# Stores moved to ScalarE's queue, other rooms for down's first left tiles, and a full-height last contraction tile

## The chip, the cores and the metric

The kernel runs on one core of one Trainium2 chip. The metric is device time in microseconds from the start to the end of the one launch; less is better. A core has five engines that work side by side and meet at semaphores: TensorE (PE, with its weight loads PEld), VectorE (DVE), ScalarE (ACT), GpSimd (POOL) and SyncE (SP), which does nothing here but start DMAs. Each engine takes its instructions in the order in which the program lists them; an instruction that has to wait holds up all that stand behind it on its engine.

## The reference

One transformer layer on a sequence of 2048 rows and 1024 columns: attention and a gated feed-forward network, each between two layer norms, each added to its input. The weights of the feed-forward network are 4-bit codes that are looked up in a table of 16 values and multiplied by a scale for each block of 64.

```
x = x + layernorm(attn(layernorm(x), Wq, Wk, Wv, Wo))       # 16 heads of 64, rotary, causal softmax
x = x + layernorm(ffn(layernorm(x), gate, up, down))

ffn(x):  W = NF4[codes] * scales          # gate, up: 2752 x 1024; down: 1024 x 2752
         inter = silu(x @ Wg.T) * (x @ Wu.T)
         return inter @ Wd.T
```

All data are float32. The dimension of 2752 is 21 tiles of 128 and one of 64.

## The kernel before

Every matrix operand is kept as a high and a low part (`split`, L119: a copy on ScalarE at L120, a subtraction on VectorE at L121), and a product is three matmuls (`mm3`, L112: high x high, high x low, low x high, L114 to L116). The order on each engine comes from a scheduler that simulates the program with its own times, not from the order of the source text. Buffers are slots of nine tags with a fixed number each (`SLOTS`, L70); a tile that wants a slot waits until the former owner's last reader is done. PSUM has eight banks in four tags.

The stages:

- Queries, keys and values are made for 8 pairs of heads and parked in memory; heads attend one after the other. For a head and a quarter J of the rows, `scores` gives unnormalized probabilities (prob, L267, L289) and `weighted` transposes them (pt, L299) and multiplies them with the values (o, L303 and L304). Its result `ol` (L306 on ScalarE, L307 on VectorE) is stored to `at[J]` at L308.
- The last pair of heads runs together with the projection by Wo. `project(t, y, beside)` handles 128 rows: it loads the attended values `af` (L435), splits them to the left operand (a2, in the views a), multiplies (pj, L445 to L447) and copies the result to `y` (L448). `residual` (L450) loads x, normalizes y (L144, on ScalarE), adds it to x on GpSimd (L455), stores the sum to `x1d` (L456) and normalizes it again into y (L144). `project_out` stores that to `yd[t]` (L475); `fill_x2` (L477) loads it back, transposes it and splits it to the operand of the gate and up products. There are 16 row tiles; the first four are done beside the attention.
- `looked_up` (L486) turns codes into weights: it loads a tile of codes (L494) and two of scales (L495, L496), converts (L499), draws five lines through the codes on ScalarE (L504, L506) and combines them on VectorE (L510 to L514). In the projection it is called for the first gate and up tiles with its codes in the single buffer of tag "ol" and its scales in "t2". Later the two share a slot of tag "pw" (3 slots of 4 KB).
- Gate and up: 22 tiles of the inner dimension times four quarters of the rows. `gate_up` (L554) makes two products in PSUM banks, Silu on ScalarE (L574), the product with up on VectorE (L575), and sums and differences on GpSimd (L587 to L595) for a Strassen-Winograd scheme of 7 products, all stored. The last of the 22 tiles has 64 rows; the other half of its tile is set to zero (L573). `down_weights` does the like for the looked-up down weights (L611 zeroes, L614 stores).
- Down: the 7 products, each 11 contraction tiles (kt) times 8 banks (r). `fetch` (L651) loads a left tile `ast` (L654) and, for every second kt, a right tile `bst` (L660), and splits both. In the last product the last four contraction tiles are held back, so that the eight banks end one after the other; `evict` (L700) and `finish` (L682) add, normalize and store. The `finish` calls of the last but one product load their rows of `x1d` (L685) into "pw".

All DMAs are started by SP (`load`, L61), stores too. A store that waits for its data so holds up the loads behind it. The scheduler also lets a DMA wait for the DMA eight places before it.

The rows that the last contraction tile uses before the change (L732, L667):

```python
rows = D if kt == half - 1 and b in ("B21", "B22", "T4") else P
...
a = ab[0][:rows, :, r // 4, r % 4 * P : (r % 4 + 1) * P]
mm3(o, a, ab[1][:rows], first, last)
```

Of the kernel before, what the change touches and what calls it, by code (L numbers as in the profile page):

```python
# [10 lines left out]
F32 = mybir.dt.float32  # L11
# [11 lines left out]
D = 64  # L23
I = 2752
P = 128
KE = E // P
# [31 lines left out]
def block_kernel(ctx, tc, x, wq, wk, wv, wo, gu_codes, gu_scales, d_codes, d_scales, cos_sin, out):  # L58
    nc = tc.nc
    V, A, G, T = nc.vector, nc.scalar, nc.gpsimd, nc.tensor  # L60
    load = nc.sync.dma_start  # L61

    const = ctx.enter_context(tc.tile_pool(name="const", bufs=1))
    small = ctx.enter_context(tc.tile_pool(name="small", bufs=4))
# [9 lines left out]
    def slot(tag, shape, dtype, name):  # L74
        assert int(np.prod(shape[1:])) * 4 <= SLOTS[tag][1] * 1024, (tag, shape)
        return sb.tile(shape, dtype, tag=tag, name=name, bufs=SLOTS[tag][0])

    def bank(tag, name="bk"):
        return ps.tile([P, 512], F32, tag=tag, name=name, bufs=BANKS[tag])
# [3 lines left out]
    def any_bank():  # L83
        turn[0] += 1
        return bank(BANK_ORDER[turn[0] % 8])
# [26 lines left out]
    def mm3(o, w, xx, first, last):  # L112

        r = T.matmul(o, lhsT=w[:, 0], rhs=xx[:, 0], start=first, stop=False)  # L114
        T.matmul(o, lhsT=w[:, 0], rhs=xx[:, 1], start=False, stop=False)  # L115
        T.matmul(o, lhsT=w[:, 1], rhs=xx[:, 0], start=False, stop=last)  # L116
        return r

    def split(hi, lo, src):  # L119
        A.copy(hi, src)  # L120
        V.tensor_tensor(lo, src, f32(hi), ALU.subtract)  # L121

    def ln_stats(row):
        st = small.tile([P, 2, 6], F32, tag="st", name="st")
        for i in range(2):
            V.bn_stats(st[:, i, :], row[i])
        return ln_rest(st)

    def ln_rest(st):
        mv = small.tile([P, 2], F32, tag="mv", name="mv")  # L130
        V.bn_aggr(mv, st.rearrange("p a b -> p (a b)"))
        ve = small.tile([P, 1], F32, tag="ve", name="ve")
        V.tensor_scalar(ve, mv[:, 1:2], EPS, None, ALU.add)
        rs = small.tile([P, 1], F32, tag="rs", name="rs")
        G.tensor_tensor(rs, ve, nhalf, ALU.pow)
        nb = small.tile([P, 1], F32, tag="nb", name="nb")
        V.tensor_scalar(nb, mv[:, 0:1], rs, -1.0, ALU.mult, ALU.mult)
        return mv[:, 0:1], rs, nb

    def halves(row):  # L140
        return row[:, :512], row[:, 512:]

    def normalize(dst, src, stats):
        A.activation(dst, src, AF.Identity, bias=stats[2], scale=stats[1])  # L144
# [12 lines left out]
    yd = [dram.tile([P, E], F32, tag=f"yd{t}", name=f"yd{t}") for t in range(NT)]  # L157
# [3 lines left out]
    at = [dram.tile([E, 512], F32, tag=f"at{c}", name=f"at{c}") for c in range(NC)]  # L161
    x1d = dram.tile([S, E], F32, tag="x1d", name="x1d")
    half = NIT // 2
# [44 lines left out]
    def prep_qkv(m, tags=("w", "w", "w")):  # L208
        return [prep_w(w, m, sc, tag) for w, sc, tag in zip((wq, wk, wv), (0.125, 1.0, 1.0), tags)]
# [82 lines left out]
    def weighted(h, J, prob, v):  # L292
        o = bank("O", "o")
        nk = 4 * J + 4
        for kb in range(nk):
            j0 = max(0, kb - 4 * J)
            pt = bank("T", "pt")
            for j in range(j0, 4):
                T.transpose(pt[:, j * P : (j + 1) * P], prob[kb // 4][:, j, kb % 4 * P : (kb % 4 + 1) * P], ident)  # L299
            cs = slice(j0 * P, 512)  # L300
            pw = slot("pw", [P, 2, 512], FR, "pw")
            split(pw[:, 0, cs], pw[:, 1, cs], pt[:, cs])
            T.matmul(o[:, cs], lhsT=v[:, kb, :], rhs=pw[:, 0, cs], start=kb == 0, stop=False)  # L303
            T.matmul(o[:, cs], lhsT=v[:, kb, :], rhs=pw[:, 1, cs], start=False, stop=kb == nk - 1)  # L304
        ol = slot("ol", [D, 512], F32, "ol")
        A.copy(ol, o[D:P, :])  # L306
        V.tensor_tensor(ol, o[:D, :], ol, ALU.add)  # L307
        load(at[J][h * D : (h + 1) * D, :], ol)  # L308

    def load_kv(h, k, v, cs):  # L310

# [11 lines left out]
    def early(f, *args):  # L323
        tc.trace_state.cur_priority -= EARLY
        r = f(*args)
        tc.trace_state.cur_priority += EARLY
        return r

    xs = [early(make_x, 0)]
    first = [early(prep_qkv, 0), prep_qkv(1, ("pa", "pa", "pb"))]  # L330
# [23 lines left out]
    def attend(h, J, q, k, v, anchors):  # L354
        weighted(h, J, scores(J, q, k, anchors), v)
# [76 lines left out]
    def project(t, y, beside):  # L432

        af = slot("f4", [P, KE, P], F32, "af")
        load(af, at[t // 4][:, t % 4 * P : (t % 4 + 1) * P].rearrange("(k p) n -> p k n", p=P))  # L435
        if beside:
            a2 = [slot("f4", [P, KE, P], FR, "a2") for _ in range(2)]
        else:
            a2 = slot("pa" if t % 2 else "hd", [P, 2, KE, P], FR, "a2")
            a2 = [a2[:, 0], a2[:, 1]]  # L440
        split(*a2, af)
        for n in range(2):
            o = bank("F" if beside else "FSS"[(2 * t + n) % 3], "pj")
            for k in range(KE):
                T.matmul(o, lhsT=a2[0][:, k], rhs=wot[k][n][:, 0], start=k == 0, stop=False)  # L445
                T.matmul(o, lhsT=a2[0][:, k], rhs=wot[k][n][:, 1], start=False, stop=False)  # L446
                T.matmul(o, lhsT=a2[1][:, k], rhs=wot[k][n][:, 0], start=False, stop=k == KE - 1)  # L447
            A.copy(y[:, n * 512 : (n + 1) * 512], o)  # L448

    def residual(t, y, xt):  # L450

        rows = slice(t * P, (t + 1) * P)
        load(xt, x[rows, :])
        normalize(y, y, ln_stats(halves(y)))
        G.tensor_tensor(xt, xt, y, ALU.add)  # L455
        load(x1d[rows, :], xt)  # L456
        normalize(y, xt, ln_stats(halves(xt)))

    x2, x2t = {}, {}

# [10 lines left out]
    def project_out(t, beside):  # L471
        y = slot("pb" if beside else "pw", [P, E], F32, "y")
        project(t, y, beside)
        residual(t, y, slot("f4" if beside else "pb", [P, E], F32, "x1"))
        load(yd[t], y)  # L475

    def fill_x2(t):  # L477
        y = slot("pw", [P, E], F32, "y")
# [3 lines left out]
    for t in range(BESIDE):  # L482
        project_out(t, True)
# [50 lines left out]
    for t in range(BESIDE, NEWX):  # L534
        project_out(t, False)
# [5 lines left out]
    for t in range(NEWX, NT):  # L541
        project_out(t, False)
        if fills:
            fill_x2(fills.pop(0))
        if t >= 10 and steps:
            steps.pop(0)()
# [101 lines left out]
    LAST = 4  # L648
    quarter, b_tile = {}, {}

    def fetch(a, b, kt):  # L651

        st = slot("f4", [P, 2, 512], F32, "ast")
        load(st, aq[a][kt])  # L654
        ta = slot("hd", [P, 2, 2, 512], FR, "at")
        split(ta[:, 0], ta[:, 1], st)
        if kt % 2 == 0:
            n = min(2, half - kt)
            st = slot("pb", [P, 2, 512], F32, "bst")[:, :n]
            load(st, bq[b][:, kt : kt + n])  # L660
            b_tile[b] = slot("w", [P, 2, 2, 512], FR, "bt")
            split(b_tile[b][:, 0, :n], b_tile[b][:, 1, :n], st)
        return ta, b_tile[b][:, :, kt % 2]

    def down(o, ab, r, rows, first, last):

        a = ab[0][:rows, :, r // 4, r % 4 * P : (r % 4 + 1) * P]  # L667
        mm3(o, a, ab[1][:rows], first, last)

    def quarters(name, tag):  # L670
        for _ in range(2):
            t = slot(tag, [P, 4, 512], F32, name)
            quarter.setdefault(name, []).extend([t[:, i] for i in range(4)])
# [51 lines left out]
    for n, (a, b) in enumerate(PRODUCTS):  # L725
        os = [any_bank() for _ in range(8)]
        if n in (0, 1, 3, 4):
            quarters(*(("u", "xc"), ("c", "xc"), None, ("v", "pa"), ("d", "pa"))[n])
        final, held = n == len(PRODUCTS) - 1, []
        for kt in range(half):  # L730
            ab = fetch(a, b, kt)
            rows = D if kt == half - 1 and b in ("B21", "B22", "T4") else P  # L732
            if final and kt >= half - LAST:
                held.append((ab, rows))
                continue
            for r in range(8):
                down(os[r], ab, r, rows, kt == 0, kt == half - 1)
        for r in range(8):
            for i, (ab, rows) in enumerate(held):
                down(os[r], ab, r, rows, False, i == LAST - 1)  # L740
            evict(n, r, os[r])


# [47 lines left out]
```

## Time and profile before

| what | us |
|---|---|
| median of 3 runs | 3069.32 (3069.14, 3069.32, 3074.55) |
| profiled execution | 3075.66 |
| its span in the trace | 3073.8 |
| mean granted clock of TensorE in it | 0.982 of full |

The profile is of one execution, not of the median one. Of the DMA issues that the change touches, the page gives these (data, queue, count, size of one, median time from issue to landing):

```profile
ast<-A SPq DMA_DIRECT2D x33, 512.0 KB, 4.4
```

and for the stretch of the last pair and the projection, 1360 to 1720 us:

```profile
x1d<-x SPq DMA_DIRECT2D x16, 512.0 KB, 4.3
yd<-y SPq DMA_DIRECT2D x16, 512.0 KB, 3.0
...
at<-ol SPq DMA_DIRECT2D x9, 128.0 KB, 2.7
```

In lines of engines, "x" gives the number of instructions merged into one row, the square brackets the idle time of the engine just before it and what ended that. SPq is the queue of SP.

### The profile page before, as it was taken

The numbers are of one execution on the slowest core, as the hardware profiler recorded it, in microseconds if no ns is written. First come the engines' busy times: TensorE is split into PE (matmuls) and PEld (weight loads), VectorE is DVE, ScalarE is ACT, GpSimd is POOL, SyncE is SP. The second block draws the span as 40 slices with busy tenths as digits, with TensorE's granted clock in tenths as the row PEclk, the third lists the DMA queues.
The fourth block names the chain that finished last, engine by engine and source line by source line (L and its number), as shares of the span: only waits on it lengthen the run. The fifth ranks groups of instructions, "written<-read, shape, count | busy, mean of one in ns | idle before, by whom it ended". The sixth has DMA issues, their size and how long they took to land.

```text
span 3073.8 us, 42810 instructions
## 1 busy us (share of the span) xinstructions
PE 2958.1 (96%) x14424; PEld 2426.6 (79%) x14424; DVE 2045.6 (67%) x3920; ACT 1700.1 (55%) x3565; POOL 960.4 (31%) x1055
## 2 busy tenths in 40 slices
PE   7979999999999999999989999999999999999998
PEld 6868888787777787777778788888888888788886
DVE  7556778777777777777565577766666677344347
ACT  3246667676666666666554466555555566332234
POOL 5334444344434343445323112222112223100034
PEclk9989999999999999999999999999999999999999
DMA  8776665747656558463346444344334444644446
GB/s 307 259 223 219 225 217 170 221 151 194 188 182 186 152 199 260 132 198 108 114 152 209 138 143 148 132 136 142 120 133 137 136 153 148 237 140 151 147 141 229
DMA packets 271739, 536.02 MB, mean 174 GB/s; under 512 B 22944, under 2 KB 113056, under 8 KB 255648
## 3 DMA queue, kind: packets, MB, share of 16 engines
q1 hardware_dynamic: 271520, 533.29, 53.8%
q8 instruction: 114, 1.87, 0.2%
q14 instruction: 105, 0.86, 0.1%
HBM read 371.98 MB, written 161.22 MB: 173 GB/s over the span
## 4 chain that ended last, share of the span: by engine, by line
PE 83%; DMA 8%; DVE 4%; ACT 2%; issue 1%; POOL 1%; SPq 1%; POOLq 0%; ACTq 0%; DVEq 0%
PE bk L114 14%; PE bk L115 14%; PE bk L116 14%; PE pt L299 6%; PE qkv L114 6%; PE qkv L115 5%; PE qkv L116 5%; PE o L304 4%; PE s L260 3%; PE o L303 3%; PE s L262 3%; DMA wf<-in_wq 1%; PE pj L445 1%; PE pj L447 1%; PE pj L446 1%
## 5 line engine op out<-in xcount | busy, mean ns | idle before, releaser
L115 PE MATMUL bk<-x,wt 128*128 128x512 f32 x1376 | 536.1, 390 | 0.0
L116 PE MATMUL bk<-x,wt 128*128 128x512 f32 x1376 | 535.8, 389 | 0.0
L114 PE MATMUL bk<-x,wt 128*128 128x512 f32 x1376 | 534.5, 390 | 0.9 <-ACT wt L120 0.9
L289 POOL TENSOR_SCALAR prob<-prob,rc 128x512 f32<-128x512 f32 (+3 forms) x640 | 405.4, 654 | 407.5 <-DVE rc L284 238.8
L267 ACT ACTIVATE prob<-s,mxs 128x512 f32<-128x512 f32 (+3 forms) x640 | 400.9, 629 | 159.1 <-DVE mxs L266 144.8
L121 DVE TENSOR_TENSOR pw<-pt,pw 128x512 fp32r<-128x512 f32 (+3 forms) x640 | 377.4, 602 | 131.2 <-ACT pw L120 129.5
L266 DVE TENSOR_REDUCE mxs<-s 128x1 f32<-128x512 f32 (+3 forms) x640 | 380.0, 602 | 100.5 <-PE s L262 60.2
L506 ACT ACTIVATE ln<-cs,bias 128x512 f32<-128x512 f32 x520 | 359.7, 716 | 109.4 <-DVE m L513 23.0
L120 ACT CAST pw<-pt 128x512 fp32r<-128x512 f32 (+3 forms) x640 | 323.1, 525 | 164.2 <-PE pt L299 134.9
L299 PE MATMUL pt<-ident,prob 128*128 128x128 f32 x2176 | 346.5, 276 | 3.2 <-DVE pw L121 3.0
L299 PEld LDWEIGHTS pt<-ident,prob 128*128 128x128 f32 x2176 | 267.9, 142 | 57.3 <-issue 4.4
L260 PE MATMUL s<-k,q 128*128 128x512 f32 (+3 forms) x640 | 268.7, 420 | 38.1 <-ACT prob L267 36.2
L114 PEld LDWEIGHTS bk<-x,wt 128*128 128x128 f32 x1376 | 258.8, 188 | 55.4 <-ACT wt L120 1.7
L116 PEld LDWEIGHTS bk<-x,wt 128*128 128x128 f32 x1376 | 258.5, 188 | 54.1 <-DVE wt L121 0.5
L115 PEld LDWEIGHTS bk<-x,wt 128*128 128x128 f32 x1376 | 258.6, 188 | 53.7
L304 PE MATMUL o<-pw,v 128*128 128x512 f32 (+3 forms) x640 | 250.3, 393 | 5.3 <-DVE pw L121 4.7
L303 PE MATMUL o<-pw,v 128*128 128x512 f32 (+3 forms) x640 | 246.7, 386 | 4.6 <-ACT pw L120 3.7
L114 PE MATMUL qkv<-xc,w 128*128 128x512 f32 x576 | 237.0, 411 | 13.6 <-ACT w L178 9.1
L114 PE MATMUL bk<-bt,at 128*128 128x512 f32 (+1 forms) x616 | 242.1, 395 | 4.3 <-ACT in L574 4.1
L115 PE MATMUL bk<-bt,at 128*128 128x512 f32 (+1 forms) x616 | 240.7, 391 | 0.0
L116 PE MATMUL bk<-bt,at 128*128 128x512 f32 (+1 forms) x616 | 239.8, 391 | 0.0
L262 PE MATMUL s<-k,q 128*128 128x512 f32 (+3 forms) x640 | 238.6, 374 | 0.0
(145 smaller groups left out, 5478.9 us busy)
## 6 DMA issues: line engine op xcount, KB each, us to landing
xc<-xd SPq DMA_DIRECT2D x96, 1024.0 KB, 8.9
q<-qs SPq DMA_DIRECT2D x128, 256.0 KB, 7.0
ast<-S SPq DMA_DIRECT2D x44, 512.0 KB, 4.0
cs<-in_gu_scales SPq DMA_DIRECT2D x172, 128.0 KB, 3.2
cs<-in_gu_codes SPq DMA_DIRECT2D x86, 256.0 KB, 2.9
A<-in SPq DMA_DIRECT2D x66, 256.0 KB, 2.1
S<-in SPq DMA_DIRECT2D x66, 256.0 KB, 3.1
ast<-A SPq DMA_DIRECT2D x33, 512.0 KB, 4.4
```

The source lines that it names most:

```text
L114: r = T.matmul(o, lhsT=w[:, 0], rhs=xx[:, 0], start=first, stop=False)
L115: T.matmul(o, lhsT=w[:, 0], rhs=xx[:, 1], start=False, stop=False)
L116: T.matmul(o, lhsT=w[:, 1], rhs=xx[:, 0], start=False, stop=last)
L121: V.tensor_tensor(lo, src, f32(hi), ALU.subtract)
L260: mm = T.matmul(s, lhsT=q[:, 0, j * P : (j + 1) * P], rhs=k[:, b:e], start=True, stop=False)
L266: V.tensor_reduce(mx, s, AX.X, ALU.max, negate=True)
L267: A.activation(prob[i][:, j, : e - b], s, AF.Exp, bias=mx, accum_out=sums[:, j % BATCH, i : i + 1])
L289: G.tensor_scalar(p, p, rc[:, jj % BATCH, i : i + 1], 0.0, ALU.mult, ALU.add)
L299: T.transpose(pt[:, j * P : (j + 1) * P], prob[kb // 4][:, j, kb % 4 * P : (kb % 4 + 1) * P], ident)
L303: T.matmul(o[:, cs], lhsT=v[:, kb, :], rhs=pw[:, 0, cs], start=kb == 0, stop=False)
L304: T.matmul(o[:, cs], lhsT=v[:, kb, :], rhs=pw[:, 1, cs], start=False, stop=kb == nk - 1)
L506: A.activation(ln, c8, AF.Prelu, bias=bias_of[ab], scale=ab[0], alpha=ab[2])
```

## The change

It has three parts. The stores of the projection (x1d, yd) and those of the attended values of the last two heads are started by ScalarE's queue; the store of x1d moves behind the second normalization in the source text. The first three left tiles of the first down product are loaded into slots of tag "pw" instead of "f4". The last contraction tile of down always uses all 128 rows, of which 64 are zeros in the short one.

```diff
-    load = nc.sync.dma_start
+    load, store = nc.sync.dma_start, nc.scalar.dma_start
...
-        load(at[J][h * D : (h + 1) * D, :], ol)
+        (store if h >= 2 * KE - 2 else load)(at[J][h * D : (h + 1) * D, :], ol)
...
         G.tensor_tensor(xt, xt, y, ALU.add)
-        load(x1d[rows, :], xt)
         normalize(y, xt, ln_stats(halves(xt)))
+        store(x1d[rows, :], xt)
...
         residual(t, y, slot("f4" if beside else "pb", [P, E], F32, "x1"))
-        load(yd[t], y)
+        store(yd[t], y)
...
-        st = slot("f4", [P, 2, 512], F32, "ast")
+        st = slot("pw" if a == "A11" and kt < 3 else "f4", [P, 2, 512], F32, "ast")
...
-    def down(o, ab, r, rows, first, last):
-
-        a = ab[0][:rows, :, r // 4, r % 4 * P : (r % 4 + 1) * P]
-        mm3(o, a, ab[1][:rows], first, last)
+    def down(o, ab, r, first, last):
+
+        mm3(o, ab[0][:, :, r // 4, r % 4 * P : (r % 4 + 1) * P], ab[1], first, last)
...
-            rows = D if kt == half - 1 and b in ("B21", "B22", "T4") else P
             if final and kt >= half - LAST:
-                held.append((ab, rows))
+                held.append(ab)
                 continue
             for r in range(8):
-                down(os[r], ab, r, rows, kt == 0, kt == half - 1)
+                down(os[r], ab, r, kt == 0, kt == half - 1)
         for r in range(8):
-            for i, (ab, rows) in enumerate(held):
-                down(os[r], ab, r, rows, False, i == LAST - 1)
+            for i, ab in enumerate(held):
+                down(os[r], ab, r, False, i == LAST - 1)
             evict(n, r, os[r])
```

On the queues, 40 DMAs go from SP to ScalarE: 8 of the attended values, 16 of x1d, 16 of yd. The scheduler lays out the work of all engines anew around the projection and around the start of down.

## The prediction

> **What bounds the kernel now.** I read the page first (busy shares, the 40 slices), then the busy time of each engine by stage, then, inside the stages that the diff touches, the instructions of TensorE in order of time with the idle time before each, and last the chain of waits and the queues of SP and ScalarE around each hole.
>
> The page's first two parts, and the busy time by stage (stretch, length, then busy microseconds and instructions of PE, PEld, DVE, ACT and POOL, then clock, DMA share, GB/s):
>
> ```profile
> span 3073.8 us, 42810 instructions
> ...
> PE 2958.1 (96%) x14424; PEld 2426.6 (79%) x14424; DVE 2045.6 (67%) x3920; ACT 1700.1 (55%) x3565; POOL 960.4 (31%) x1055
> ```
>
> ```profile
> 1360.00:1720.00 360.00, 330.48 (x1622) 269.59 (x1621) 229.06 (x507) 212.83 (x427) 123.03 (x126) 0.96 0.46 152
> 1720.00:2540.00 820.00, 820.00 (x3619) 679.00 (x3618) 560.81 (x828) 455.76 (x713) 171.11 (x111) 1.00 0.41 135
> 2540.00:2660.00 120.00, 114.75 (x490) 93.16 (x489) 80.22 (x100) 63.67 (x91) 36.93 (x27) 0.97 0.62 211
> 2660.00:3050.00 390.00, 390.00 (x1712) 319.84 (x1711) 177.31 (x208) 124.30 (x140) 46.73 (x36) 1.00 0.50 158
> ```
>
> TensorE is the bound: it is never idle through the gate and up products and through the down products. So a cover elsewhere is worth nothing; only its holes, its clock and its own instructions count. Its holes lie where the diff works: 29.5 us in the last pair and the projection (1360 to 1720), 5.3 us where down begins (2540 to 2660). The largest, from the instructions of TensorE in order of time (start, length, instruction, idle before it and its releaser):
>
> ```profile
> 1573.99 0.80 PE L445 MATMUL pj<-wo,a 128*128 128x512 f32 x1 [3.84 <-ACT y L448]
> 1589.71 0.79 PE L445 MATMUL pj<-wo,a 128*128 128x512 f32 x1 [6.24 <-ACT a L120]
> 2643.06 0.80 PE L114 MATMUL bk<-bt,at 128*128 128x512 f32 x1 [4.14 <-ACT in L574]
> 2643.65 0.63 PE L115 MATMUL bk<-bt,at 128*128 128x512 f32 x1
> ```
>
> After such a hole the next matmuls start 0.43 us apart instead of 0.227: between 2643.06 and 2648.34 there are 12 of them, 5.28 us in place of 2.72, so the hole costs another 2.6 us.
>
> Third, the starts inside down, where one product changes to its 64-row tile and back:
>
> ```profile
> 2754.34 0.39 PE L116 MATMUL bk<-bt,at 128*128 128x512 f32 x1
> 2754.65 0.49 PE L114 MATMUL bk<-bt,at 64*128 64x512 f32 x1
> 2754.99 0.39 PE L115 MATMUL bk<-bt,at 64*128 64x512 f32 x1
> 2755.22 0.39 PE L116 MATMUL bk<-bt,at 64*128 64x512 f32 x1
> ```
>
> Starts that should be 0.227 apart are 0.31 and 0.34 apart: a change of row count costs 0.2 us, although no idle time is shown. Last, the queue of SP in the projection (who waited for whom, total us, times, longest) and the chain of waits behind the three holes (start, length, what):
>
> ```profile
> SPq L475 <- ACT y L144: 51.8, 11, 7.4
> SPq L308 <- DVE nb L137: 32.2, 1, 32.2
> SPq L308 <- DVE ol L307: 29.0, 5, 12.7
> SPq L456 <- POOL x L455: 24.8, 11, 7.8
> ```
>
> ```profile
> 1565.68 5.91 DMA cs<-in_gu_codes
> ...
> 1581.23 4.22 DMA cs<-in_gu_codes
> ```
>
> ```profile
> 2619.67 5.30 DMA bst<-B
> ...
> 2627.38 3.59 DMA bst<-B
> ...
> 2633.33 6.46 DMA bst<-B
> ```
>
> SP stands some 138 us in front of stores with loads behind them, but the two holes of the projection end on code tables: ScalarE stands in order before a lookup line (L506), and evictions (L448) and left-tile copies (L120) stand behind it. The hole at 2643 ends on the third right tile of down (bst): its copy L120 holds up the last Silu (L574), which must free a PSUM bank.
>
> **What the Trainium skill says.** "DMA: Bandwidth & Descriptors", section "Issuing engines are not separate DMA queues": starting DMAs from several engines saves only the sequencer's time to start them. Agrees as far as it can be seen: a store takes SP 0.32 to 0.57 us. "TensorE: Matmul & The Clock Gate", section "What's actually happening": after an idle window of about 3.4 us the array runs at half clock until it was busy as long. The trace agrees: 0.43 for 0.227 after 4.14 us idle, while the stretch 1480 to 1500, with a hole of 1.65 us, shows clock 1.00. "TensorEngine Tiling (Array Packing)", section "Key Properties": a change of tiling mode drains TensorE. I read a 64-row matmul between 128-row ones as such a change; the 0.2 us fit[...]; here the 64-row L115 takes 388 ns, the 128-row one 389.
>
> **The change, part by part.**
>
> *128 rows for the last contraction tile.* 3 products x 8 x 3 = 72 matmuls keep their length and lose the changes. In the second product and in the sixth the tile comes once for all eight r: one change in, one out, 2 x 0.2 = 0.4 us each. In the last product four tiles are held back and each r goes through 128, 128, 128, 64: its rounds start 3.15 us apart where 12 x 0.227 = 2.72 would do, 0.43 each, 7.5 rounds = 3.2 us. Sum 4.0. The rows added were set to zero before being stored (L573, L611), so no instruction is added. At the end the eight finishes must follow faster: VectorE does 2.4 to 3.1 us per round, so it may lag; I give back 0.4. Value -3.6, ends -4.1 and -2.0.
>
> *The first three left tiles of down in the lookups' rooms (pw).* In the new order of SP they take the places of the three x1 loads (L685, at 2601.6, 2606.1 and 2611.6 before), and these follow. So three loads and splits leave the crowded 2618 to 2636 (DMA share 0.79 to 0.96). Against it: one split is put inside the last lookup on VectorE (1.23 us) and ScalarE (1.05), and SP now waits with its third x1 load until the third tile is split (landing near 2616.5, copies until 2618.8) with T4, S4 and the first right tile behind it: that goes out near 2621.8 in place of 2619.67. Then each right tile needs its load, 1.05 of ScalarE and 1.23 of VectorE before the next may enter the one free pb room: 2629, then 2635.4, landing near 2640 if the load takes 4.5 us and not 6.46. Its copy, then L572 and L574 (0.58 and 0.59) end near 2642. TensorE gets there, as before, at 2638.9. So the hole shrinks by 1 to 2 us, to a length at which the clock may or may not drop (2.6 us). Value -2.2; ends -7.1 (hole and clock loss gone) and +2 (the chain of right tiles late by the whole 2.1 us).
>
> *The stores.* 8 at L308 (heads 14 and 15, four J), 16 at L456 and 16 at L475, 40 DMAs, go from SP's queue to ScalarE's, each with its wait. Issue: 40 x 0.36 = 14 us on ScalarE, which is busy 213 of 360 us; beside TensorE's work except in the chain to the two holes. The waits: L308 for VectorE's sum, 0.7 us; L475 for ScalarE's own L144, nothing; the x1d store for POOL's L455, 2.4 us after L144. Behind it stand ScalarE's casts and evictions, and TensorE for those. In the new order it mostly has lookup lines or evictions ahead of it, or the second L144 behind it, which waits for that sum anyway.
> What is gained: in the chain to 1573.99 the fifth line of the first lookup now comes before the two L144 (2.28 us), so the next codes can go out at 1563.5 and not 1565.68; but a third line (0.7) and a store (0.35) now come before the eviction. Net -1.3 at the first hole. At the second, two L144 and one store more stand before the copy of the left tile, but the whole lookup ahead of it is earlier by some 4 us; I take another -1.3. The rest of the codes' wait stays: their room is one buffer, freed only by the last line. Holes between 1490 and 1515 (1.65, 0.58, 1.70): the left tiles' f4 rooms are freed by TensorE, not by SP, so -0.4. The holes at 1704 to 1710 (1.34, 0.79, 2.22) wait for splits of the last normalized rows, whose loads stood behind the last yd store (1692.62): -1.0. Sum -4.0. Ends: -15.7 (both large holes, 10.1, and two clock losses, 5.2, with 0.4 more) and +10 (rival below).
>
> Sum -3.6 - 2.2 - 4.0 = -9.8. The profiled execution took 3075.66 (span 3073.8 and 1.9 around it) and would take 3065.9; it lies 6.3 above the median of the runs, 3069.32, so the forecast on the median is 3059.5.
>
> **Rivals.** *Everything opens*: without stores SP feeds both lookups early enough and down starts without a stop: -15.7, -7.1 and -4.1, 3042. For it: 138 us of SP's waits. Against: the codes' room and the pb room are not SP's matter. *Only the row change counts*: holes move and keep their size, -3.6, 3065.7, too little to be told from no change. For it: ScalarE's order holds the same lines before the same copies. *Slower*: x1d stores block ScalarE. Some of them (t = 8 and 10, nearly so 13) stand directly behind the L144 whose sum they await, with transposes' copies behind them; 2.5 us each, and from 1600 to 1700 TensorE has almost no hole now (0.56 us). If ten of the projections lose 2.5 us and 60% reaches TensorE through full transpose banks, +15, less the -5.8 of the other two parts: 3078.5. It decides from the point where these holes pass some 12 us in sum. Against: evictions have three banks and 5.4 us per half row tile.
>
> **How the numbers follow.** 0.2%, 6.1 us, is what a measurement of this kernel can tell. Forecast (3054 to 3063) 0.53; everything opens (below 3054) 0.15; only the row change (3063 to 3070) 0.15; slower 0.17, of it 0.03 within 0.2%. So faster 0.68, same 0.18, slower 0.14. Range 3046 to 3072: below it only the far end of the first rival, above it two thirds of the last.
>
> **What would show it.** Right: starts at the last tile 0.227 apart and rounds of 2.72 us in the last product; a hole before the eighth bank of down under 3.5 us; holes near 1574 and 1590 still there but smaller by some 2.6 us in sum; SP without waits on L144. Wrong: holes from 1600 to 1700 behind copies that stand behind a store; the first right tile later than 2623; an end after the last matmul longer by over 2 us, which would mean that the finishes, not the matmuls, set the end.

## The result, and the profile after

| | before | after |
|---|---|---|
| median, us (runs) | 3069.32 (5 runs, 3064.85 to 3075.65) | 3085.6 (5 runs, 3076.7 to 3086.57) |
| ratio after/before, 95% interval | | 1.0042 (1.0022 to 1.0062) |
| profiled execution: span, us | 3073.8 | 3083.8 |
| granted clock | 0.982 | 0.981 |

The changed kernel is slower by 0.42% in the mean of its runs, some 13 us (the medians lie 16 apart); forecast was 9.8 us faster, and the range ended at 3072. The busy time by stage of the changed kernel (stretch, length, then busy time and instructions of PE, PEld, DVE, ACT, POOL, then clock, DMA share, GB/s) shows the two places that the prediction worked on:

```profile
1360.00:1720.00 360.00, 317.67 (x1554) 256.76 (x1553) 212.60 (x482) 201.28 (x401) 120.18 (x124) 0.95 0.46 149
2540.00:2660.00 120.00, 111.29 (x481) 90.78 (x481) 77.82 (x98) 61.04 (x89) 35.65 (x26) 0.97 0.56 186
```

TensorE does 317.67 us in the last pair and the projection where it did 330.48, and 111.29 where down begins in place of 114.75. (These stretches are fixed in time and so don't hold quite the same work: the kernel of the first experiment below, whose projection is unchanged, does 326.40 in the first.) Its instructions in order of time (start, length, instruction, idle before it and its releaser) say where the holes are:

```profile
1569.51 0.50 PE L445 MATMUL pj<-wo,a 128*128 128x512 f32 x1 [3.30 <-ACT y L448]
...
1582.49 1.94 PE L151 MATMUL pt<-ident,y 128*128 128x128 f32 x8 [5.62 <-DMA y<-yd]
1587.04 0.80 PE L445 MATMUL pj<-wo,a 128*128 128x512 f32 x1 [2.61 <-ACT a L120]
...
1649.08 1.94 PE L151 MATMUL pt<-ident,y 128*128 128x128 f32 x8 [7.57 <-DMA y<-yd]
...
2656.73 0.79 PE L114 MATMUL bk<-bt,at 128*128 128x512 f32 x1 [7.61 <-ACT in L574]
```

The first hole is 3.30 where it was 3.84. Forecast was 1.3 less; five traces with the projection of before (named below) show 3.40 to 4.22 there, so little of it is left. The second has another owner: TensorE first waits for rows that are read back from memory (y<-yd), and only then, more briefly, for a left tile. The hole of 7.57 at 1649 is new; at that place the kernel before stood 0.56 us, and the five traces show 0.56 to 2.46. The hole of down grew from 4.14 to 7.61. Only the last product went as forecast: its last three matmuls start 0.23 apart, with no other form among them.

```profile
3071.75 0.39 PE L114 MATMUL bk<-bt,at 128*128 128x512 f32 x1
3071.98 0.39 PE L115 MATMUL bk<-bt,at 128*128 128x512 f32 x1
3072.20 0.39 PE L116 MATMUL bk<-bt,at 128*128 128x512 f32 x1
```

Medians of this kernel move by several us from one set of runs to the next, and the traces show a part of it: one and the same matmul near 1380 (L303, 128x128) starts between 1375.56 and 1387.76 in the traces of kernels whose edits all lie behind it. So I cut each span at four events of TensorE: that matmul; the end of the last transposes of rows read back (L151, near 1710); the arrival at the hole of down (the start of the matmul behind it less its idle time); the start of the last matmul. Those of these lines that aren't shown above, before and then after:

```profile
1381.16 0.33 PE L303 MATMUL o<-pw,v 128*128 128x128 f32 x1 [2.85 <-ACT pw L120]
...
1709.53 0.77 PE L151 MATMUL pt<-ident,y 128*128 128x128 f32 x4 [2.22 <-DVE x L121]
...
3063.15 0.39 PE L116 MATMUL bk<-bt,at 64*128 64x512 f32 x1
```

```profile
1377.00 0.33 PE L303 MATMUL o<-pw,v 128*128 128x128 f32 x1 [3.10 <-ACT pw L120]
...
1720.14 1.06 PE L151 MATMUL pt<-ident,y 128*128 128x128 f32 x4
```

Worked out from them:

| us | up to 1380 | last pair and projection | gate, up | hole of down | down | after the last matmul |
|---|---|---|---|---|---|---|
| before | 1381.2 | 329.1 | 928.6 | 4.1 | 420.1 | 10.7 |
| after | 1377.0 | 344.2 | 927.9 | 7.6 | 415.5 | 11.6 |
| difference | -4.2 | +15.1 | -0.7 | +3.5 | -4.6 | +0.9 |

In five traces whose projection is that of the kernel before (its own, and four from below: the 128 rows alone, the left tiles' rooms alone, these with GpSimd's order held, and the right tiles in pw rooms), this stage takes 327.2 to 333.6 us, 329.9 in the mean, and the idle times of TensorE in it sum to 25.5 to 28.7; in the changed kernel they sum to 38.0. Against that mean the projection lost 14.3, down's beginning 3.5, and the last tile brought 3.7 (4.6 less 0.9).

### The profile page after: what moved, and what is told of

It reads as the page before. It is cut to its first block, busy times and chain, and to the rows that moved or that the text cites. A ratio compares the mean times of both kernels' runs of the same rounds, so it can differ in the third digit from the quotient of the medians.

```text
span 3083.8 us, 42799 instructions
## 1 busy us (share of the span) xinstructions
PE 2953.7 (96%) x14424; PEld 2427.1 (79%) x14424; DVE 2045.1 (66%) x3920; ACT 1700.9 (55%) x3565; POOL 960.0 (31%) x1055
## 4 chain that ended last, share of the span: by engine, by line
PE 79%; DMA 10%; DVE 5%; ACT 2%; issue 2%; POOL 1%; SPq 1%; POOLq 0%; ACTq 0%; DVEq 0%
PE bk L114 13%; PE bk L115 13%; PE bk L116 13%; PE pt L299 6%; PE qkv L114 5%; PE qkv L116 5%; PE qkv L115 5%; PE o L304 4%; PE s L260 3%; PE o L303 3%; PE s L262 3%; DMA xc<-xd 1%; DMA wf<-in_wq 1%; PE pj L445 1%; PE pj L446 1%
## 5 line engine op out<-in xcount | busy, mean ns | idle before, releaser
L121 DVE TENSOR_TENSOR pw<-pt,pw 128x512 fp32r<-128x512 f32 (+3 forms) x640 | 377.2, 601 | 125.7 <-ACT pw L120 123.9
L303 PE MATMUL o<-pw,v 128*128 128x512 f32 (+3 forms) x640 | 246.9, 387 | 4.7 <-ACT pw L120 4.1
L114 PE MATMUL bk<-bt,at 128*128 128x512 f32 x616 | 239.9, 391 | 7.6 <-ACT in L574 7.6
L115 PE MATMUL bk<-bt,at 128*128 128x512 f32 x616 | 240.8, 391 | 0.8 <-DVE bt L121 0.8
L116 PE MATMUL bk<-bt,at 128*128 128x512 f32 x616 | 239.7, 391 | 0.0
```

## The experiments

Each comparison is with runs of the kernel before on the same chip, whose median lay between 3071.4 and 3074.8; 0.1% is 3.1 us.

**The three parts alone.** The rows edit as in the change:

```diff
-            rows = D if kt == half - 1 and b in ("B21", "B22", "T4") else P
-                down(os[r], ab, r, rows, kt == 0, kt == half - 1)
+                down(os[r], ab, r, kt == 0, kt == half - 1)
```

> Only the last contraction tile over 128 rows is taken from the change. Theory A (each part acts alone: rows gain, stores and rooms lose): 3 to 4 us faster, about 3065.5 against 3069; in the last product rounds of 2.72 us and starts 0.227 apart, nothing else moves before 2740 us. Theory B (the row changes cost nothing that reaches the end, since the finishes set it): no change in time, and the idle time after TensorE's last matmul longer by 3 us. If it is slower, the profile's 0.2 us for a change of row count was read wrongly.

Ratio 0.9987 (0.9977 to 0.9996): 4 us faster. Seven rounds of the last product, from the starts of its last 85 matmuls, take 19.04 us where they took 22.07 before, 2.72 each in place of 3.15. Down takes 415.7 in place of 420.1, the end after the last matmul 11.15 in place of 10.65. Theory A.

The rooms of the left tiles:

```diff
-        st = slot("f4", [P, 2, 512], F32, "ast")
+        st = slot("pw" if a == "A11" and kt < 3 else "f4", [P, 2, 512], F32, "ast")
```

> Only the rooms of down's first three left tiles are taken from the change. Theory A (SP's queue: the x1 loads and left-tile splits now stand ahead of the right tiles): 3 to 5 us slower, about 3073, with the hole before the eighth bank of down at 7 us or more in place of 4.14 and the first right tile some 5 us later than 2619.67. Theory B (that delay in the changed kernel came from the stages before, not from the rooms): no change or up to 3 us faster, hole under 4.2 us.

Ratio 1.0012 (1.0003 to 1.0021), 3.7 us slower. The trace shows the chain, from all engines in order of time; gate and up end some 4.5 us earlier in it than in the trace of before (TensorE reaches the hole at 2634.42 and not at 2638.92):

```profile
2602.34 1.84 POOL L623 TENSOR_TENSOR mb<-mb 128x512 f32<-128x512 f32 x1
2602.94 2.32 DVE L121 TENSOR_TENSOR at<-ast,at 128x1024 fp32r<-128x1024 f32 x1
...
2608.28 0.68 DVE L514 TENSOR_TENSOR mb<-mb,cs 128x512 f32<-128x512 f32 x1
...
2608.44 2.82 POOL L591 TENSOR_TENSOR in<-in 128x512 f32<-128x512 f32 x1 [2.02 <-DVE in L575]
2608.88 1.21 DVE L121 TENSOR_TENSOR at<-ast,at 128x1024 fp32r<-128x1024 f32 x1
...
2611.31 0.52 POOL L611 MEMSET mb<- 64x512 f32 x1
2612.17 0.41 SPq L614 DMA_DIRECT2D B<-mb  x1
2618.09 1.29 POOL L629 TENSOR_TENSOR mb<-mb 128x512 f32<-128x512 f32 x1 [4.00 <-DMA B<-mb]
2621.06 0.38 SPq L660 DMA_DIRECT2D bst<-B  x1
...
2642.11 0.80 PE L114 MATMUL bk<-bt,at 128*128 128x512 f32 x1 [7.69 <-ACT in L574]
```

The same steps before:

```profile
2611.69 0.52 POOL L611 MEMSET mb<- 64x512 f32 x1 [1.40 <-DVE mb L514]
2612.24 0.32 SPq L614 DMA_DIRECT2D B<-mb  x1
2612.30 1.62 POOL L591 TENSOR_TENSOR in<-in 128x512 f32<-128x512 f32 x1
...
2616.50 1.28 POOL L629 TENSOR_TENSOR mb<-mb 128x512 f32<-128x512 f32 x1 [1.21 <-DMA B<-mb]
```

The split of a left tile (L121, the part on VectorE), put inside the last lookup, takes 2.32 us in place of the usual 1.21, with GpSimd's subtractions (L623 and the next) beside it. The lookup (its last line is L514) ends 1.9 us later against TensorE's arrival at the hole (25.46 us ahead of it, 27.35 before). GpSimd is then in a sum of the gate tiles (L591), which the scheduler had put behind the zeroing (L611) before; the store of B21 goes out 4.4 us late, lands in 5.9 us in place of 4.26 (why, stays open: an x1 load of 512 KB went out shortly ahead of it in both kernels), and the first right tile goes out 5.9 us late (13.36 us ahead of TensorE's arrival, 19.25 before). Two more right tiles hang on it, through one free room.

All stores on ScalarE's queue, without the other two parts:

```diff
-        load(at[J][h * D : (h + 1) * D, :], ol)
+        (store if h >= 2 * KE - 2 else load)(at[J][h * D : (h + 1) * D, :], ol)
...
-        load(x1d[rows, :], xt)
         normalize(y, xt, ln_stats(halves(xt)))
+        store(x1d[rows, :], xt)
...
-        load(yd[t], y)
+        store(yd[t], y)
```

> Only the moved stores are taken from the change (all three kinds, with the x1d store behind the second normalization). Theory A (the stores make all of the loss in the projection): 10 to 15 us slower, about 3081, with a hole of 5 to 8 us near 1650 in front of the transposes of rows read back from yd, and down beginning as in the kernel before (hole about 4.1 us). Theory B (the loss is shared between the parts or is a matter of single executions): at most 5 us slower and no hole over 3 us between 1600 and 1700.

Ratio 1.0039 (1.0024 to 1.0055), 12 us slower; last pair and projection 343.1 us, hole of down 3.37. The same new hole stands in front of the transposes:

```profile
1593.54 1.94 PE L151 MATMUL pt<-ident,y 128*128 128x128 f32 x8 [5.51 <-DMA y<-yd]
...
1660.82 1.94 PE L151 MATMUL pt<-ident,y 128*128 128x128 f32 x8 [7.94 <-DMA y<-yd]
```

The three parts sum to -4.0 + 3.7 + 12.0 = 11.7 us, the whole change measured 13 (6.8 to 19): they add, as far as the intervals tell. What remains is why the stores cost so much.

**Which stores.** One kind at a time, the edits as above.

> Only the stores of yd (16) go to ScalarE's queue; those of the last attended values and of x1d stay with SP, x1d in its old place. Theory A1 (a yd store on ScalarE's queue lands late, 6.3 us in place of 3.0, and the load of the same row behind it makes TensorE wait): most of the loss of all stores, 8 to 13 us slower, with the hole at 1650. Theory A2 (the x1d store stands in ScalarE's order or in the queue in front of yd and is what delays it): at most 3 us slower here, no hole over 4 us between 1600 and 1700.

> Only the stores of the last pair's attended values (8) go to ScalarE's queue. Theory A1 (what costs is a store of yd that shares the transfers with SP's loads): these are 128 KB and early, so no change within 3 us. Theory A2 (anything that stands in ScalarE's order delays the evictions): 3 to 5 us slower, and with the others' shares the sum of 12.

> Only the x1d stores (16) go to ScalarE's queue, behind the second normalization in the text. Theory A1 (the landing of yd counts, and yd stays in SP's queue in front of the next x load): no change or up to 3 us slower, no hole over 4 us between 1640 and 1660. Theory A2 (the x1d store in ScalarE's order, waiting for GpSimd's sum, is what makes the rows late): 4 to 8 us slower, with second normalizations later by some 5 us against the matmuls of their tile.

| stores on ScalarE's queue | ratio (interval) | us | last pair and projection, us |
|---|---|---|---|
| yd | 1.0014 (1.0003 to 1.0025) | +4.3 | 336.6 |
| at | 1.0009 (1.0000 to 1.0018) | +2.8 | 332.1 |
| x1d | 0.9995 (0.9981 to 1.0009) | -1.5 | 327.6 |
| all | 1.0039 (1.0024 to 1.0055) | +12 | 343.1 |

The x1d stores, whose wait for GpSimd's sum was the rival of the prediction, cost nothing that can be told when they are moved alone (by the interval at most 2.8 us). That rival falls. The yd stores cost most, but 4.3 lies between the "8 to 13" of A1 and the 3 of A2; the hole in front of the transposes is 4.57 us near 1644 in their trace. The three single kinds sum to 5.6 of 12 (by the stages to 6.6 of 13.2). That points to something that appears only with all of them, but the intervals together (some 7.7 us) allow none.

**How a store of yd can hold up TensorE.** The load y<-yd that TensorE waits for reads a row that was stored long ago. (`fill_x2` runs seven row tiles behind `project_out`.) But its room is one of three (tag pw) that it shares with the rows being projected, and the room comes free only when the yd store of such a row has landed. All engines in order of time, the kernel before, then the changed one:

```profile
1639.10 0.32 SPq L475 DMA_DIRECT2D yd<-y  x1
1639.53 0.37 SPq L453 DMA_DIRECT2D x<-in_x  x1
...
1642.08 0.32 SPq L479 DMA_DIRECT2D y<-yd  x1
...
1646.23 0.52 PE L151 MATMUL pt<-ident,y 128*128 128x128 f32 x3 [0.56 <-DMA y<-yd]
```

```profile
1639.62 0.33 SPq L453 DMA_DIRECT2D x<-in_x  x1
1639.63 0.36 ACTq L475 DMA_DIRECT2D yd<-y  x1
...
1645.82 0.32 SPq L479 DMA_DIRECT2D y<-yd  x1
```

Before, store and load of 512 KB stand one behind the other in one queue, 0.43 us apart: the store lands in 2.9 us and the read of the next row goes out at once. After, they start 0.01 us apart on two queues, and the issue table for each of the two gives 6.1 us for the store and 5.9 for the load. The read goes out 6.2 us after the store and not 3.0. That is 3.2 us; counted from the matmul near 1380, the store itself goes out 4.7 us later (1639.63 less 1377.00, before 1639.10 less 1381.16), so the read is 7.9 late, and the landing of this store is less than half of that. From 1590 to 1720 the medians (issue, queue, count, size, us to landing) are, before and after:

```profile
yd<-y SPq DMA_DIRECT2D x9, 512.0 KB, 2.9
x<-in_x SPq DMA_DIRECT2D x7, 512.0 KB, 4.1
```

```profile
yd<-y ACTq DMA_DIRECT2D x9, 512.0 KB, 5.1
x<-in_x SPq DMA_DIRECT2D x7, 512.0 KB, 5.9
```

The Trainium skill gives a reason in "DMA: Bandwidth & Descriptors", section "Queues, rings and completion order": each DMA engine goes in turn, packet by packet, between the queues that have work. The two transfers of a pair would so end together, late. The trace agrees: 6.1 and 5.9 beside each other, 2.9 for the one that went first in one queue.

**The x loads on the same queue.** If that is the cause, the pair must be put in one queue again, whichever:

```diff
-        load(xt, x[rows, :])
+        (store if t >= NEWX else load)(xt, x[rows, :])
```

> The moved stores, and with them the x loads of the tiles from 7 on: these go to ScalarE's queue too, behind the yd store of the tile before, so that the two no longer run side by side on two queues. Theory A1 (a yd store beside an x load takes 6 us in place of 3, its room comes free that much later, and the row read into the room arrives late): yd stores land in about 3 us again, the hole in front of the transposes near 1650 (7.94 us in the kernel with the stores moved) shrinks to under 5, and 3 to 6 us of the 12 come back. Theory A2 (the delay is ScalarE's order, not the landing): yd lands sooner but the hole stays over 6 us and the time within 2 us of the kernel with the stores moved.

Ratio 1.0015 (1.0007 to 1.0023): of 12 us, 7 came back (by the stages 9.2 of 13.2). yd lands in 2.9 us, x in 4.2, the hole near 1650 is gone, the largest one there is now 1.24 near 1632, and the stage takes 333.9 us. But the scheduler also made another order for it, so it doesn't show that landing alone did this. The counter-test is the kernel before with the x loads alone on ScalarE's queue:

> The kernel before with one edit: the x loads of the tiles from 7 on go to ScalarE's queue, all stores stay with SP. Nothing waits for a store in ScalarE's order, and TensorE's order up to the last tile is that of the kernel before. Theory A1 (a yd store and an x load that start together on two queues take twice as long each): yd lands in 4.5 to 6 us in place of 2.9, a hole of 3 to 7 us appears in front of the transposes near 1646, 3 to 7 us slower. Theory A2 (it needs the stores in ScalarE's order): no change within 2 us.

Ratio 1.0004 (0.9993 to 1.0015), no change that can be told; a hole of 1.27 near 1643, within the 0.56 to 2.46 of the five traces. Theory A1 as I put it fails here: yd lands in 3.7 us in the median, not 4.5 to 6. From 1590 on, stores that ScalarE's x load followed by 0.30 to 0.50 us took 3.0 to 3.7 us, and those issued at the same time as the load 4.3 to 5.1. So a landing longer by 1.4 to 2.2 us for four of the stores cost nothing that can be told. Longer landings of single stores don't explain the 12 us alone.

**Queue against order.** The order on every engine comes from a scheduler that simulates the program, so a store on another queue also moves TensorE's, ScalarE's and VectorE's work. To tell the two apart I held the instructions of one kernel, from the last pair to the end of the projection, in the order of the other, with order edges that wait for nothing (one chain for each engine, and one for SP's loads):

```diff
+    for engine, runs in ORDERS.items():
...
+                    dep = mybir.DependencyInfo(mybir.DependencyClass.NoSync, mybir.DependencyReason.DATA)
+                    tc.add_manual_dep(i, last.name, dep, reason="order")
```

> The stores moved as in the change, but TensorE's, ScalarE's, VectorE's and GpSimd's instructions and SP's loads held, from the last pair of heads to the end of the projection, in the order of the kernel before; the stores fall where the scheduler puts them on ScalarE. Theory Q (the second queue itself: yd stores and x loads side by side, waits of stores in front of ScalarE's work): most of the 12 us stays, 8 to 12 us slower than before, yd landing in 5 to 6 us, hole near 1650. Theory O (the scheduler's new order, which puts the second normalization of the tiles from 8 on behind evictions and casts, makes the rows late): at most 4 us slower than before.

> The other way round: all stores on SP's queue, but the same instructions held in the order that the scheduler made for the moved stores. Theory Q: at most 4 us slower than before, yd landing in 2.9 us. Theory O: 8 to 12 us slower, hole near 1650. If both this and the run before are slow by some 6, the two add.

| | SP's queue | ScalarE's queue |
|---|---|---|
| order of before | 1 (stage 329.9, mean of five) | 1.0019 (1.0007 to 1.0031), +5.8 us (stage 337.5) |
| order made for the moved stores | 1.0029 (1.0014 to 1.0043), +8.9 us (stage 338.5) | 1.0039 (1.0024 to 1.0055), +12 us (stage 343.1) |

Neither theory alone. The queue costs 5.8 us with the old order (7.6 by the stage); the order costs 8.9 with the old queue (8.6); with both, 12 (13.2). Each is clear of no change; which of the two is larger can't be told. With the queue and the old order, the medians from 1590 to 1720 are:

```profile
yd<-y ACTq DMA_DIRECT2D x10, 512.0 KB, 5.1
x<-in_x SPq DMA_DIRECT2D x8, 512.0 KB, 4.9
```

So the late landing comes with the queue and doesn't need the new order: SP waits 29.5 us for yd stores there before it can send out reads, 17.5 before. The same trace has other costs of the queue: near 1492 a left tile's copy waits 2.52 us for its load, and TensorE's hole behind it is 3.13, in the five traces 1.34 to 1.74. How much of the 5.8 is the landing isn't parted. With the order and the old queue, the stores stand among SP's loads again, whose order was made without them (from 1360 to 1720 the four largest waits in front of them sum to 156 us, 138 before); a part of the 8.9 may be that. TensorE in order of time with the new queue and the old order (lines are 14 higher in these two kernels), then with the old queue and the new order:

```profile
1587.49 1.94 PE L165 MATMUL pt<-ident,y 128*128 128x128 f32 x8 [4.09 <-DMA y<-yd]
1594.45 0.80 PE L459 MATMUL pj<-wo,a 128*128 128x512 f32 x1 [5.03 <-ACT a L134]
...
1654.24 1.07 PE L165 MATMUL pt<-ident,y 128*128 128x128 f32 x8 [2.34 <-DVE a L135]
```

```profile
1585.08 1.94 PE L165 MATMUL pt<-ident,y 128*128 128x128 f32 x8 [6.26 <-DMA y<-yd]
1590.44 0.79 PE L459 MATMUL pj<-wo,a 128*128 128x512 f32 x1 [3.43 <-ACT a L134]
...
1650.53 1.94 PE L165 MATMUL pt<-ident,y 128*128 128x128 f32 x8 [5.04 <-DMA y<-yd]
```

The hole near 1650 is 0.56 to 2.46 with neither, 2.34 with the queue, 5.04 with the order, 7.57 and 7.94 with both: in these traces it grows only with the order, while with the queue alone other holes do (31.3 us in sum, against 25.5 to 28.7). With the new order and the old queue, the ninth row tile's yd store goes out 243.7 us after the matmul near 1380 (1625.31 less 1381.63), before 238.9 (1620.06 less 1381.16): 4.8 us late. Of these, 3.6 are there already at its first normalization (1615.27 and 1611.23 by the same count); the rest falls between the two, where ScalarE's new order has two evictions of a later tile and two casts of weights. That store is no mark of the order alone, though: with the queue and the old order it goes out later still, after 244.8 us (1626.32 less 1381.52). Which single move in the new order costs how much wasn't tried.

**The rooms: is it GpSimd's order?** The left tiles in pw rooms, and L591 of the last gate tiles held behind the zeroing L611, as before:

```diff
-            G.memset(m[rows:], 0.0)
+            zeroed[:] = [G.memset(m[rows:], 0.0)]
...
-            G.tensor_tensor(first[:, 1], first[:, 1], second[:, 1], ALU.add)
+            sums = G.tensor_tensor(first[:, 1], first[:, 1], second[:, 1], ALU.add); zeroed and after(sums, zeroed[0])
```

> The rooms of the first three left tiles as in the change, but on GpSimd the first sum of the last gate tiles (L591) is held behind the zeroing of the last looked-up down weights (L611), as in the kernel before. Theory B1 (the split put inside the last lookup delays it, GpSimd then takes the 2.8 us sum first, and the store of B21, the sum T4 and the first right tile go out 5.6 us late): two to three of these 5.6 us come back, the hole before the eighth bank of down is 4 to 6 us in place of 7.69. Theory B2 (SP's x1 loads ahead of the right tile are the cause): hole still over 7 us.

Ratio 1.0011 (1.0002 to 1.0021), which can't be told from 1.0012. In the trace the hole is 6.58 in place of 7.69, outside what both theories expected. The B21 store is 1.9 us late and not 4.4, but the first right tile still 4.5 (14.72 us ahead of TensorE's arrival). GpSimd's order is worth 1.1 us of the hole in these two traces, which is less than the hole varies where the start of down is unedited (3.14 to 4.97 in ten traces); the rest lies with the split in the lookup and with what stands on SP in front of the right tile (x1 loads, left tiles and the S4 store), which B2 named. I didn't part these two.

**Versions that might beat both.** The pb room that right tiles pass on can be avoided: give the three pw rooms to the right tiles.

```diff
-            st = slot("pb", [P, 2, 512], F32, "bst")[:, :n]
+            st = slot("pw" if a == "A11" and kt < 6 else "pb", [P, 2, 512], F32, "bst")[:, :n]
```

> The 128-row tile, and the rooms of tag pw given to down's first three right tiles in place of its first three left tiles; stores as before. If the hole before the eighth bank of down hangs on the one free pb room that passes from right tile to right tile: hole under 1 us and no slow matmuls behind it, 5 to 7 us less than with the rows alone, 9 to 11 less than before (about 3060). If it hangs on ScalarE's and VectorE's splits or on the left tiles: hole 2 to 4 us, and at most 2 us less than the rows alone.

> As the one with 128 rows and pw rooms for the right tiles, and the x1d stores on ScalarE's queue behind the second normalization. The x1d stores alone were 1.5 us faster with an interval that held zero: 0 to 2 us less than without them.

The first, with the 128-row tile: ratio 0.9984 (0.9974 to 0.9994), 4.9 us faster than before. With the x1d stores on ScalarE's queue as well: 0.9982 (0.9975 to 0.9989), 5.5 faster. TensorE's instructions behind the hole, in the first:

```profile
2645.31 0.50 PE L114 MATMUL bk<-bt,at 128*128 128x512 f32 x1 [1.53 <-ACT in L574]
2645.64 0.40 PE L115 MATMUL bk<-bt,at 128*128 128x512 f32 x1
2645.88 0.39 PE L116 MATMUL bk<-bt,at 128*128 128x512 f32 x1
2646.11 0.39 PE L114 MATMUL bk<-bt,at 128*128 128x512 f32 x1
```

The hole is 1.53 in place of 4.03 with the rows alone, and the matmuls behind it are 0.23 apart at once: down takes 413.3 us in place of 415.7. That is 4.9 us; the end after the last matmul takes 1.1 more, so 3.8 are left by the stages. The ratios show 0.9 of it, within their intervals. Expected were 5 to 7 and a hole under 1 us: in these two traces the room was the larger part of the hole, and not all of it. The x1d stores add nothing that can be told. Both beat the kernel before; neither, as estimated, by more than 0.2%.

## Why the prediction was wrong, step by step

- **128 rows: right.** Forecast -3.6, measured -4.0 (-7.1 to -1.2) and by the stages -3.9. Rounds went from 3.15 to 2.72 and the end took 0.5 longer where 0.4 had been given back.
- **Left tiles in pw rooms, value -2.2: wrong sign.** Measured +3.7. The step that failed is "that goes out near 2621.8 in place of 2619.67", 2.1 us late; it was 5.9 with the rooms alone, and 4.9 in the changed kernel (2634.76, which is 14.36 us ahead of TensorE's arrival). The prediction saw the split inside the last lookup, priced it at 1.23 and stopped there. It took 2.32 and delayed the store of B21; the scheduler put GpSimd's next sum in front of that store, and the store took 1.6 us longer to land. How the delay divides between these and SP's loads stays open. The far end of +2, "the chain of right tiles late by the whole", was the right chain and too short.
- **Stores, value -4.0: wrong sign and size.** Measured +12. Two steps failed. "L475 for ScalarE's own L144, nothing" looked at when a store is issued, and not at when it lands and who waits for its room; SP's loads then ran beside it, yd landed in 5.1 us in place of 2.9, and that queue cost 5.8 (not all of it need be the landing). And the order was read for the instructions near the holes of before alone; the whole of the new one cost 8.9 on the old queue, and which move in it does so stays open. The holes near 1574 and 1590 were to shrink by 2.6 in sum; they are 11.5 with the transposes' new hole, and 10.1 to 11.7 in the five traces.
- **The rival "Slower"** had the right side and, with 3078.5, some 7 us too little, by the wrong mechanism, so that it came near was luck: x1d stores alone made the kernel no slower. That holes from 1600 to 1700 would show the forecast wrong did come true; they end on a read-back, not on copies behind a store. Its sign of a first right tile later than 2623 came true too (4.9 us late, as above).
- **The sums of the ends** have two slips that didn't move the forecast: a hole of 4.14 and a clock loss of 2.6 make 6.7, not 7.1, and the stores' end of +10 is less than the +15 that the rival reckons with.
- **"Everything opens" and "Only the row change counts"** both took holes for things that shrink or stay. The holes of the projection grew, from 25.5 to 38.0 in sum.

## What to carry to other kernels

When a store is moved to another queue, ask not only who issues it but what it overtook in the old one: a store that frees a room, sent ahead of a large load in one queue, landed here in 2.9 us, and beside that load on a second queue in 5 to 6. Follow each moved instruction to the next owner of its buffer, and compare the whole order of every engine up to there, since a scheduler that reorders can cost as much as the edit (here 8.9 and 5.8 us, with intervals that overlap). Where the unchanged part of a program varies by more than the effect, compare stages between events of the same engine, not spans.

## What had not been expected of the hardware

- Two transfers of 512 KB that start within 0.01 us on two queues took 5.9 and 6.1 us; in one queue, 0.43 apart, 2.9 and 3.9. In pairs that start within 0.02 us, yd stores took 4.8 to 7.1 us on ScalarE's queue and 3.9 to 5.1 on SP's (the run that moved only x loads). A lead of some 0.3 us on two queues is not sure to help: such stores took 3.3, 3.5, 3.7 and 4.2 us, and 5.6 twice.
- A VectorE subtraction of two SBUF tiles (L121) took 2.32 us beside GpSimd's subtractions, and 1.21 elsewhere in the same trace; a GpSimd sum (L591) took 2.82 beside such a subtraction, which itself kept its 1.21, and 1.27 later. The Trainium skill, "SBUF — State Buffer", section "SBUF: two separate sides", says that the two share a port pair as an exclusive lock; these numbers agree with it: one of the two waits, and the split of 2.32 us ends 1.1 us, about its usual length, after the GpSimd instruction beside it (L623, 2602.34 to 2604.18).
- The same unchanged stage up to the matmul near 1380 took from 1375.56 to 1387.76 us in the executions of different kernels. What varies in it wasn't looked into.
